# A decoder layer on one core: value products of the self attention in bursts of eight, divisions two runs at a time

## The chip, the cores and the metric

The kernel runs on one NeuronCore of a Trainium2 chip. The metric is the time of one execution on the device in microseconds (us), as the median of several runs; less is better.

The names of the engines in the profile: PE is TensorE (matmuls), PEld its weight loads, DVE is VectorE, ACT is ScalarE, POOL is GpSimd, SP is SyncE, which here issues DMAs.

## The reference

One decoder layer on `x` of shape (4, 1024, 256): a self attention block with residual and layer norm, a cross attention block over 154 context rows with residual and layer norm, and a mixture of 8 experts with a shared expert, residual and layer norm. The change lies in the first attention inside the self attention block:

```python
q = (hidden_states @ Wq + bq).reshape(b, s, NH, HD).transpose(0, 2, 1, 3)
k = (hidden_states @ Wk + bk).reshape(b, s, NH, HD).transpose(0, 2, 1, 3)
v = (hidden_states @ Wv + bv).reshape(b, s, NH, HD).transpose(0, 2, 1, 3)
scores = jnp.einsum('bhqd,bhkd->bhqk', q, k) / jnp.sqrt(jnp.asarray(HD, q.dtype))
mod = jax.nn.sigmoid(hidden_states @ cg_W + cg_b + (cons_vec @ am_W + am_b))
scores = scores * mod.transpose(0, 2, 1)[..., None]
probs = jax.nn.softmax(scores, axis=-1)
ctx = jnp.einsum('bhqk,bhkd->bhqd', probs, v).transpose(0, 2, 1, 3).reshape(b, s, h)
causal_ctx = _mha(hidden_states, hidden_states, ca_Win, ca_bin, ca_Wout, ca_bout, CAUSAL_HEADS)
ctx = ctx * (1.0 - CAUSAL_W) + causal_ctx * CAUSAL_W
meta_ctx = _mha(ctx, ctx, mc_Win, mc_bin, mc_Wout, mc_bout, META_HEADS)
ctx = ctx * (1.0 - META_W) + meta_ctx * META_W
return ctx @ Wo + bo
```

There are 16 heads of 16 features, 1024 queries and 1024 keys per batch, and 4 batches. All is in float32.

## The kernel before, in words

The four batches go through the attention blocks one after the other; the experts follow for all tokens at the end. For each batch the first attention (class `Self`, lines 435 to 559) runs through the loop of lines 932 to 960.

Work is cut by heads and queries. Four heads make a group `g`, 256 queries a part, so a batch has 4 x 4 = 16 units `u` of one group and one part. A unit has 8 steps `s`, so the loop has 128 steps, numbered `n`. The four heads of a group lie 32 partitions apart, so that matmuls with 32 rows each can stand on separate row groups of the array.

In each step the loop does, in this order:

- `maxima(n + 12)`: two matmuls of queries against keys for two heads (L483) into a tile `big` of two PSUM banks (the pool has two such tiles), and a maximum over the keys on DVE (L490). After a unit's eighth step the two halves are joined by DVE into column 31 of each head in `mxcol` (L495); two transposes on TensorE (L397, in `maxima_rows`) turn these columns into rows, and DVE adds them to the query tile (L400), where row 31 of each head is kept for the negative maximum. The lead of 12 steps is done ahead, in `begin`, for the first steps of a batch.
- `exponentials(n)`: four matmuls of keys against queries (L521) for two heads and 256 keys. In even steps they go into two tiles of the pool `one` (three banks), in odd steps into one of these and the single bank `acc`. ACT takes the exponential of each bank (L532) into a tile `ex`. In the last 12 steps of a batch, where there are no maxima left to make, the scores use a `big` tile instead and ACT takes both banks at once (L529).
- in some steps a piece of other work (projections of the next attention, or the end of the previous batch), and then `clock.step()`.

`Clock` keeps a list of pieces that are due: `later(2, f)` runs `f` at the end of the next step, `later(1, f)` at the end of the present one. Three kinds of pieces go through it: the transposed maxima (`rows`), the value products (`product`) and the divisions (`divide`).

The value product (L541) has the weights `v`, 128 keys by 32 columns for a head, 16 features and a column of ones that gives the sum of the exponentials. The four heads write to four column groups of one `one` bank. Before the change a burst covers the exponentials of four steps: 4 chunks of 128 keys by 4 heads, 16 matmuls, behind the steps 3 and 7 of a unit. ACT copies the bank (L549), and for the second half POOL adds the first half to it (L554). Two steps later `divide` transposes the sum (L405, two transposes for 256 queries), and DVE takes the reciprocal of the sums and multiplies (L408, L409).

The tile framework sets semaphores between the engines and places the instructions of each engine in an order of its own, which can differ a little from the order of the program's lines. For example, in the built order one of the two L483 matmuls of a step stands in front of a burst of L541, and the other behind it, once in nearly every unit.

Each matmul in float32 shows as two records in the profile, so `x32` at L541 is a burst of 16.

Of the kernel before, what the change touches and what calls it, by code (L numbers as in the profile page):

```python
# [8 lines left out]
F32 = mybir.dt.float32  # L9
# [3 lines left out]
ALU = mybir.AluOpType  # L13
# [3 lines left out]
P = 128  # L17
# [7 lines left out]
QW = 256  # L25
NG = NH // 4
MH, MD = 4, 64
MR = 31
# [18 lines left out]
def decoder_layer(ctx: ExitStack, tc: tile.TileContext, a, out):  # L47
    nc = tc.nc
# [10 lines left out]
    def big():  # L59
        return pbig.tile([P, 2, 512], F32, tag="big", name="big")  # L60

    def small():
        return pone.tile([P, 512], F32, tag="one", name="one")

    def acc():
        return pacc.tile([P, 512], F32, tag="acc", name="acc")
# [139 lines left out]
    with tc.tile_pool(name="wA", bufs=1) as wA, tc.tile_pool(name="work", bufs=2) as work:  # L206
# [111 lines left out]
        def ex_tile(shape, name):  # L318
            return work.tile(shape, F32, tag="ex", name=name, bufs=EXB)
# [72 lines left out]
        def maxima_rows(mx, q):  # L392

            n = mx.shape[1]
            ps = small()
            for t in range(n):
                nc.tensor.transpose(  # L397
                    ps[:, t * P : (t + 1) * P], mx[:, t].rearrange("p j w -> p (j w)"), ident
                )
            nc.vector.tensor_tensor(q, ps[:, 0 : n * P], q, ALU.add)  # L400

        def divide(avs, g, t0, n, ctok):
            ps = small()
            for t in range(n):
                nc.tensor.transpose(ps[:, t * P : (t + 1) * P], avs[:, t * P : (t + 1) * P], ident)  # L405
            pv = ps[:, 0 : n * P].rearrange("p (t j w) -> p t j w", t=n, w=32)
            rs = work.tile([P, 4, 4], F32, tag="rs", name="rs")
            nc.vector.reciprocal(rs[:, 0:n], pv[:, :, :, HD])  # L408
            nc.vector.tensor_tensor(  # L409
                ctok[:, t0 : t0 + n, g * 64 : (g + 1) * 64].rearrange(  # L410
                    "p t (j d) -> p t j d", d=HD
                ),
                pv[:, :, :, 0:HD],
                rs[:, 0:n].unsqueeze(3).to_broadcast([P, n, 4, HD]),
                ALU.mult,
            )
# [18 lines left out]
        class Self:  # L435
# [35 lines left out]
            def maxima(self, n):  # L471
                u, s = divmod(n, 8)
                g, part = divmod(u, 4)
                st = self.st[g]
                t, kb, pair = s // 4, (s // 2) % 2, s % 2
                if s == 0:
                    st["mxp", part] = work.tile([P, 2, 2, 4], F32, tag="mxp", name="mxp")
                mxp = st["mxp", part]
                ps = big()
                for jj in range(2):  # L480
                    r = 32 * (2 * pair + jj)
                    tok = part * QW + t * P
                    nc.tensor.matmul(  # L483
                        ps[:, jj, :],
                        st["q"][r : r + MR, tok : tok + P],
                        st["k"][r : r + MR, kb * 512 : (kb + 1) * 512],
                        start=True,
                        stop=True,
                    )
                nc.vector.reduce_max(mxp[:, t, kb, 2 * pair : 2 * pair + 2], ps, axis=AX.X)  # L490
                if s == 7:
                    mx = mxcol[u % 2]

                    def rows():
                        nc.vector.tensor_tensor(  # L495
                            mx[:, :, :, MR], mxp[:, :, 0, :], mxp[:, :, 1, :], ALU.max
                        )
                        maxima_rows(mx, st["q"][:, part * QW : (part + 1) * QW])

                    self.clock.later(2, rows)  # L500

            def exponentials(self, n, alone):
                u, s = divmod(n, 8)
                g, part = divmod(u, 4)
                st = self.st[g]
                kcp, pair = s // 2, 1 - s % 2
                if s == 0:
                    st["ex"] = {}
                exs = st["ex"]
                ex = exs[kcp, pair] = ex_tile([P, 2, 512], "ex")  # L510

                if alone:
                    both = big()
                    scs = [both[:, 0, :], both[:, 1, :]]
                else:
                    scs = [small(), small() if s % 2 == 0 else acc()]
                for i in range(2):
                    for jj in range(2):
                        r = 32 * (2 * pair + jj)
                        kc = 2 * kcp + i  # L520
                        nc.tensor.matmul(  # L521
                            scs[jj][:, i * QW : (i + 1) * QW],
                            st["k"][r : r + MR + 1, kc * P : (kc + 1) * P],
                            st["q"][r : r + MR + 1, part * QW : (part + 1) * QW],
                            start=True,
                            stop=True,
                        )
                if alone:
                    nc.scalar.activation(ex, both, AF.Exp, scale=1.0 / HD**0.5)  # L529
                else:  # L530
                    for jj in range(2):
                        nc.scalar.activation(ex[:, jj, :], scs[jj], AF.Exp, scale=1.0 / HD**0.5)  # L532
                if s in (3, 7):

                    def product():
                        av = small()
                        for kc in range(s - 3, s + 1):
                            i = kc % 2 * QW
                            for j in range(4):
                                h = 4 * g + j  # L540
                                nc.tensor.matmul(  # L541
                                    av[32 * j : 32 * j + 32, 0:QW],
                                    self.v[:, kc, h * VW : h * VW + 32],
                                    exs[kc // 2, j // 2][:, j % 2, i : i + QW],
                                    start=(kc == s - 3),
                                    stop=(kc == s),
                                )
                        avs = work.tile([P, QW], F32, tag="avq", name="avq", bufs=3)
                        nc.scalar.copy(avs, av[:, 0:QW])  # L549
                        if s == 3:  # L550
                            st["av"] = avs
                        else:

                            nc.gpsimd.tensor_tensor(avs, avs, st["av"], ALU.add)  # L554
                            self.clock.later(
                                2, lambda: divide(avs, g, 2 * part, 2, self.ctok)
                            )

                    self.clock.later(2, product)
# [19 lines left out]
        def mha_units(qk, v, weight, cx):  # L579
# [93 lines left out]
            for u in range(n + 2):  # L673
                pss = scores(u) if u < n else None
                if 1 <= u <= n:
                    flip(u - 1, 0)
                if u < n:
                    exponentials(u, pss)
                if 1 <= u <= n:
                    flip(u - 1, 1)  # L680
                    del probs[u - 1]
                if u >= 2:
                    product(u - 2)
                yield
# [16 lines left out]
        class Cross:  # L701
# [67 lines left out]
            def product(self, n):  # L769

                g, tp = n // 8, n % 8 // 2
                av = acc()
                pts = [self.pt.pop(n - 1), self.pt.pop(n)]
                for c in range(2):
                    for j in range(4):
                        h = 4 * g + j
                        nc.tensor.matmul(  # L777
                            av[32 * j : 32 * j + 32, 0:QW],
                            self.vx[:, c, h * VW : h * VW + 32],
                            pts[j // 2][0:HK, c, j % 2 * QW : (j % 2 + 1) * QW],  # L780
                            start=(c == 0),
                            stop=(c == 1),
                        )
                avs = work.tile([P, QW], F32, tag="avq", name="avx", bufs=3)
                nc.scalar.copy(avs, av[:, 0:QW])
                self.clock.later(2, lambda: divide(avs, g, 2 * tp, 2, self.ctok))

# [130 lines left out]
        for b in range(B):  # L918
# [13 lines left out]
            for n in range(total):  # L932
                g, s = divmod(n, 32)
# [87 lines left out]
            for g in range(NG):  # L1021
                for c in range(NC2):
# [4 lines left out]
                        start=(c == 0),  # L1027
                        stop=(c == NC2 - 1),
# [10 lines left out]
            for k in range(2):  # L1039
                ps = small()  # L1040
                for c in range(NC2):
# [4 lines left out]
                        start=(c == 0),  # L1046
                        stop=(c == NC2 - 1),
# [76 lines left out]
    def k1(name, shape=(P, NTT, NE)):  # L1124
        return fw.tile(list(shape), F32, tag="k1", name=name, bufs=8)
# [84 lines left out]
    for k in range(2):  # L1210
        mine = k1("mine")
# [257 lines left out]
```

## Time and profile before

| | before |
|---|---|
| time, median of 3 runs | 3394.84 us (3393.89 to 3398.46) |
| the profiled execution's own time | 3315.92 us |
| its span | 3314.1 us |
| granted TensorE clock in it, mean | 0.985 |
| DVE busy | 1668.9 us (50%) |
| ACT busy | 1619.0 us (49%) |
| L490 DVE, maxima over keys | 512 instructions, 611.2 us, mean 1219 ns |
| L541 PE, value products | 4096 records, mean 384 ns each |
| L549 ACT, copies of products | 128 instructions, 47.6 us, mean 372 ns |
| L554 POOL, additions of halves | 64 instructions, 46.4 us, mean 725 ns |

Matmul records overlap in time: the four row groups or column groups work at once. Their durations are modelled and include the way through the array, so that the distance from one start to the next says more than a duration. A window of the profile gives the busy time of each engine in a stretch, and the granted clock, 1.00 for full speed. The self attention loop of the first batch takes from about 80 to 342 us of the span, that of the others some 260 us each from about 740, 1410 and 2080 us.

### The profile page before, as it was taken

The numbers are of one execution on the slowest core, as the hardware profiler recorded it, in microseconds if no ns is written. First come the engines' busy times: TensorE is split into PE (matmuls) and PEld (weight loads), VectorE is DVE, ScalarE is ACT, GpSimd is POOL, SyncE is SP. The second block draws the span as 40 slices with busy tenths as digits, with TensorE's granted clock in tenths as the row PEclk, the third lists the DMA queues.
The fourth block names the chain that finished last, engine by engine and source line by source line (L and its number), as shares of the span: only waits on it lengthen the run. The fifth ranks groups of instructions, "written<-read, shape, count | busy, mean of one in ns | idle before, by whom it ended". The sixth has DMA issues, their size and how long they took to land.

```text
span 3314.1 us, 60483 instructions
## 1 busy us (share of the span) xinstructions
PE 3202.8 (97%) x25064; PEld 2042.6 (62%) x25064; DVE 1668.9 (50%) x3513; ACT 1619.0 (49%) x3179; POOL 352.2 (11%) x565
## 2 busy tenths in 40 slices
PE   8999999999999999999999999999999999999997
PEld 3665667566556675665566756655667575666664
DVE  3665555556655555566545556666456553111113
ACT  1565645465655453756554537555545452233334
POOL 1000000100000001000000010000000004433331
PEclk7999999999999999999999999999999999999998
DMA  7300000101000001010000010000000016322224
GB/s 227 87 1 1 1 1 2 47 28 40 2 1 1 1 2 47 28 39 2 1 1 1 2 47 28 14 2 3 9 10 2 1 42 232 86 48 45 45 46 122
DMA packets 83768, 111.36 MB, mean 34 GB/s; under 512 B 8896, under 2 KB 69672, under 8 KB 83496
## 3 DMA queue, kind: packets, MB, share of 16 engines
q1 hardware_dynamic: 70056, 89.60, 8.6%
q0 software_dynamic: 13440, 17.90, 3.3%
q8 instruction: 200, 3.28, 0.4%
q14 instruction: 72, 0.59, 0.1%
HBM read 59.10 MB, written 48.37 MB: 32 GB/s over the span
## 4 chain that ended last, share of the span: by engine, by line
PE 84%; DVE 10%; issue 3%; ACT 2%; DMA 1%; POOL 0%; SPq 0%; ACTq 0%; DVEq 0%; POOLq 0%
PE big L483 8%; PE big L591 8%; PE big L1293 7%; PE one L627 7%; PE acc L645 7%; DVE mxp L490 7%; PE big L342 7%; PE one L541 7%; PE acc L1319 4%; PE one L521 4%; PE one L758 3%; PE one L356 3%; PE big L191 3%; PE big L723 3%; PE acc L777 2%
## 5 line engine op out<-in xcount | busy, mean ns | idle before, releaser
L490 DVE TENSOR_REDUCE mxp<-big 128x2 f32<-128x1024 f32 x512 | 611.2, 1219 | 344.4 <-PE acc L521 261.4
L483 PE MATMUL big<-k,q 31*128 31x512 f32 x2048 | 615.9, 639 | 34.2 <-DVE mxp L490 23.9
L521 PE MATMUL one<-q,k 32*128 32x256 f32 x2784 | 501.8, 398 | 0.0
L532 ACT ACTIVATE ex<-one 128x512 f32<-128x512 f32 x696 | 390.8, 600 | 218.3 <-PE acc L521 178.0
L323 DVE CUSTOM_DVE_ANT_0 prob<-big,zero_t 128x1024 f32<-128x1024 f32 x256 | 303.6, 1222 | 266.5 <-PE big L591 266.4
L521 PEld LDWEIGHTS one<-q,k 32*128 32x128 f32 x2784 | 331.3, 185 | 33.1 <-ACT ex L532 2.0
L610 ACT ACTIVATE prob<-prob,nmx 128x1024 f32<-128x1024 f32 x256 | 293.0, 1152 | 20.6 <-DVE nmx L323 20.0
L483 PEld LDWEIGHTS big<-k,q 31*128 31x128 f32 x2048 | 186.1, 188 | 175.6 <-DVE mxp L490 88.8
L632 ACT COPY pt<-one 128x512 f32<-128x512 f32 x256 | 137.8, 590 | 305.1 <-PE one L627 305.0
L591 PE MATMUL big<-mk,mq 64*128 64x512 f32 x1024 | 279.3, 623 | 2.6 <-ACT ex L529 2.6
L627 PEld LDWEIGHTS one<-ident,prob 128*128 128x128 f32 x2048 | 219.7, 141 | 96.6 <-issue 90.8
L1293 PE MATMUL big<-wall,xt 128*128 x576 | 270.5, 593 | 0.5 <-ACT xt L1272 0.5
L521 PE MATMUL acc<-q,k 32*128 32x256 f32 x928 | 263.9, 403 | 0.0
L627 PE MATMUL one<-ident,prob 128*128 128x128 f32 x2048 | 255.6, 278 | 0.0
L541 PE MATMUL one<-ex,v 128*32 128x256 f32 x4096 | 250.0, 384 | 5.0 <-DVE q L400 5.0
L1303 DVE TENSOR_TENSOR hidr<-big,slr 128x512 f32<-128x512 f32 x72 | 49.8, 692 | 364.5 <-ACT slr L1301 364.5
L743 ACT ACTIVATE xs<-xs,xmx 128x154 f32<-128x154 f32 x512 | 175.0, 413 | 105.5 <-DVE xmx L323 105.5
L541 PEld LDWEIGHTS one<-ex,v 128*32 128x32 f32 x4096 | 119.9, 110 | 138.6 <-ACT ex L532 54.0
L634 DVE COPY pt<-one 128x512 f32<-128x512 f32 x256 | 164.4, 684 | 9.1 <-PE one L627 9.1
L591 PEld LDWEIGHTS big<-mk,mq 64*128 64x128 f32 x1024 | 98.0, 188 | 100.2 <-issue 78.7
L323 DVE CUSTOM_DVE_ANT_0 xs<-big,bias 128x154 f32<-128x154 f32 x512 | 132.6, 314 | 52.8 <-PE big L723 26.7
L554 POOL TENSOR_TENSOR avq<-avq 128x256 f32<-128x256 f32 x64 | 46.4, 725 | 1050.8 <-ACT avq L549 1050.8
(261 smaller groups left out, 4695.4 us busy)
## 6 DMA issues: line engine op xcount, KB each, us to landing
scratch<-empty SPq DMA_DIRECT2D x1, 9288.0 KB
xg<-scratch SPq DMA_DIRECT2D x72, 129.0 KB
q<-q_rows SPq DMA_DIRECT2D x16, 512.0 KB
k<-k_rows SPq DMA_DIRECT2D x16, 512.0 KB
y<-in_x_dram SPq DMA_DIRECT2D x4, 1024.0 KB
q_rows<-qh SPq DMA_DIRECT2D x8, 512.0 KB
k_rows<-kh SPq DMA_DIRECT2D x8, 512.0 KB
wall<-in_L_ffn_w_gate_dram SPq DMA_DIRECT2D x8, 512.0 KB
```

The costliest lines, as they stand in the source:

```text
L323: nc.vector.tensor_tensor_reduce(out=out, in0=ps, in1=bias, scale=-1.0, scalar=3.0e38, op0=ALU.add, op1=ALU.min, accum_out=low,)
L342: nc.tensor.matmul(ps[:, tb, :], w[:, c, lo : lo + P], xT[:, c, tb * 512 : (tb + 1) * 512], start=(c == 0), stop=(c == NC2 - 1),)
L483: nc.tensor.matmul(ps[:, jj, :], st["q"][r : r + MR, tok : tok + P], st["k"][r : r + MR, kb * 512 : (kb + 1) * 512], start=True, stop=True,)
L490: nc.vector.reduce_max(mxp[:, t, kb, 2 * pair : 2 * pair + 2], ps, axis=AX.X)
L521: nc.tensor.matmul(scs[jj][:, i * QW : (i + 1) * QW], st["k"][r : r + MR + 1, kc * P : (kc + 1) * P], st["q"][r : r + MR + 1, part * QW : ...
L532: nc.scalar.activation(ex[:, jj, :], scs[jj], AF.Exp, scale=1.0 / HD**0.5)
L541: nc.tensor.matmul(av[32 * j : 32 * j + 32, 0:QW], self.v[:, kc, h * VW : h * VW + 32], exs[kc // 2, j // 2][:, j % 2, i : i + QW], start= ...
L591: nc.tensor.matmul(pss[i][:, kb, :], q[r : r + MD, t * P : (t + 1) * P], k[r : r + MD, kb * 512 : (kb + 1) * 512], start=True, stop=True,)
L610: nc.scalar.activation(p, p, AF.Exp, bias=nmx[:, i : i + 1], scale=-1.0, accum_out=sm[:, t % 4, i : i + 1],)
L627: nc.tensor.transpose(ps[:, kc * P : (kc + 1) * P], probs[u][i][:, at : at + P], ident)
L645: nc.tensor.matmul(av[64 * i : 64 * i + 64, (t % 4) * P : (t % 4 + 1) * P], v[:, kc, h * MD : (h + 1) * MD], flipped[u][i][:, kc, :], star ...
L1293: nc.tensor.matmul(ps[:, g, :], xt[:, c * P : (c + 1) * P], wall[:, bass.ds(off + (g * NC2 + c) * D, D)], start=(c == 0), stop=(c == NC2 - 1),
```

## The change

Value products now follow every odd step: `product` takes the two chunks of keys of two steps, 8 matmuls, into a bank of its own, four times in a unit. ACT copies the first of the four into its half of a tile `avq` for two parts (512 columns), the other three into tiles `avp`, which POOL adds on. `divide` runs once for two parts, with four transposes. The transposed maxima are put in the list with `later(1)` in place of `later(2)`, and the joining maximum on DVE follows its reduction at once. The copy of the cross attention (L785) changes its tag, with the same size and number of buffers.

```diff
                 if s == 7:
                     mx = mxcol[u % 2]
-
-                    def rows():
-                        nc.vector.tensor_tensor(
-                            mx[:, :, :, MR], mxp[:, :, 0, :], mxp[:, :, 1, :], ALU.max
-                        )
-                        maxima_rows(mx, st["q"][:, part * QW : (part + 1) * QW])
-
-                    self.clock.later(2, rows)
+                    nc.vector.tensor_tensor(mx[:, :, :, MR], mxp[:, :, 0, :], mxp[:, :, 1, :], ALU.max)
+                    q = st["q"][:, part * QW : (part + 1) * QW]
+                    self.clock.later(1, lambda: maxima_rows(mx, q))
...
-                if s in (3, 7):
+                if s % 2 == 1:
 
                     def product():
+
                         av = small()
-                        for kc in range(s - 3, s + 1):
-                            i = kc % 2 * QW
+                        for i in range(2):
+                            kc = 2 * kcp + i
                             for j in range(4):
                                 h = 4 * g + j
                                 nc.tensor.matmul(
                                     av[32 * j : 32 * j + 32, 0:QW],
                                     self.v[:, kc, h * VW : h * VW + 32],
-                                    exs[kc // 2, j // 2][:, j % 2, i : i + QW],
-                                    start=(kc == s - 3),
-                                    stop=(kc == s),
+                                    exs[kcp, j // 2][:, j % 2, i * QW : (i + 1) * QW],
+                                    start=(i == 0),
+                                    stop=(i == 1),
                                 )
-                        avs = work.tile([P, QW], F32, tag="avq", name="avq", bufs=3)
-                        nc.scalar.copy(avs, av[:, 0:QW])
-                        if s == 3:
-                            st["av"] = avs
-                        else:
-
-                            nc.gpsimd.tensor_tensor(avs, avs, st["av"], ALU.add)
+                        if kcp == 0 and part % 2 == 0:
+                            st["av"] = work.tile([P, 2 * QW], F32, tag="avq", name="avq", bufs=2)
+                        avs = st["av"]
+                        mine = avs[:, part % 2 * QW : (part % 2 + 1) * QW]
+                        if kcp == 0:
+                            nc.scalar.copy(mine, av[:, 0:QW])
+                            return
+                        more = work.tile([P, QW], F32, tag="avp", name="avp", bufs=3)
+                        nc.scalar.copy(more, av[:, 0:QW])
+                        nc.gpsimd.tensor_tensor(mine, mine, more, ALU.add)
+                        if kcp == 3 and part % 2 == 1:
                             self.clock.later(
-                                2, lambda: divide(avs, g, 2 * part, 2, self.ctok)
+                                2, lambda: divide(avs, g, 2 * part - 2, 4, self.ctok)
                             )
...
-                avs = work.tile([P, QW], F32, tag="avq", name="avx", bufs=3)
+                avs = work.tile([P, QW], F32, tag="avp", name="avx", bufs=3)
```

Line numbers in the text are those of the kernel before.

## The prediction

> **What bounds the kernel now.** I read the page first, then the stages in windows, then TensorE, DVE and ACT in order of time over one unit of the self attention (eight steps of the loop at lines 932 to 960).
>
> The page, on the engines' busy time:
>
> ```profile
> PE 3202.8 (97%) x25064; PEld 2042.6 (62%) x25064; DVE 1668.9 (50%) x3513; ACT 1619.0 (49%) x3179; POOL 352.2 (11%) x565
> ```
>
> The window of one unit (us, then busy PE, PEld, DVE, ACT and POOL, then the granted clock):
>
> ```profile
> 200.46:215.68 15.22, 14.48 (x170) 9.07 (x166) 10.24 (x13) 9.15 (x18) 0.73 (x1) 1.00 0.01 2
> ```
>
> The timeline (start, us, engine, line; in brackets the idle time before and what ended it):
>
> ```profile
> 208.16 0.70 PE L483 MATMUL big<-k,q 31*128 31x512 f32 x2 [0.44 <-DVE mxp L490]
> ...
> 210.37 1.93 PE L541 MATMUL one<-ex,v 128*32 128x256 f32 x32
> ...
> 212.23 0.70 PE L483 MATMUL big<-k,q 31*128 31x512 f32 x2
> ...
> 213.41 2.36 DVE L490 TENSOR_REDUCE mxp<-big 128x2 f32<-128x1024 f32 x2 [1.71 <-PE acc L521]
> 213.48 0.60 ACT L532 ACTIVATE ex<-one 128x512 f32<-128x512 f32 x1 [0.69 <-PE acc L521]
> ...
> 213.98 0.59 ACT L532 ACTIVATE ex<-acc 128x512 f32<-128x512 f32 x1
> ...
> 216.12 1.22 DVE L490 TENSOR_REDUCE mxp<-big 128x2 f32<-128x1024 f32 x1
> ...
> 217.37 0.17 DVE L495 TENSOR_TENSOR mxcol<-mxp 128x8 f32<-128x8 f32 x1
> ...
> 217.69 0.41 PE L397 MATMUL one<-ident,mxcol 128*128 128x128 f32 x2 [0.24 <-DVE mxcol L495]
> 218.03 1.12 PE L483 MATMUL big<-k,q 31*128 31x512 f32 x2
> ```
>
> The page says TensorE, and so does the unit, but its 14.48 of 15.22 us are modelled ends. The rows show the pace. A step is the maxima pair (L483) and four score matmuls (L521) on the other two row groups. Where nothing stops them, the first step behind a burst takes 0.98 us (212.23 to 213.21) and the next one 0.87. After each burst of sixteen products (L541, 210.37 to 212.23, 1.86 us) DVE has run dry (idle 1.71 us), and then TensorE waits for DVE, since the maxima have two banks (208.16). From start to start one unit is 1.08 + 1.86 + 0.98 + 1.01 + 0.47 + 1.39 + 1.61 + 0.34 + 1.05 + 1.86 + 0.98 + 1.46 + 1.13 = 15.22 us. The term 1.05 is one maxima matmul that stands alone in front of a burst (218.03 to 219.08), its partner behind it. The interval 15.22 repeats 11 to 12 times in each of four batches.
>
> **The change part by part.** In order, per unit:
>
> Products. The same 4096 records of L541, in four bursts of eight for two of sixteen. A round (a pass of 256 columns; L521's follow each other at 212.57, 212.78, 213.00) takes 0.216 us. A burst of sixteen is eight rounds plus 0.13, so one of eight is 1.00 us and two cost 0.14 more than one. Each new burst also has an entry of 0.11 (the second maxima pass at 209.83 plus 0.43 is 210.26; L541 starts at 210.37).
>
> Wait for exponentials. A burst now needs the exponentials of the step just before, which only one step of work covers. From an odd step's start (212.23) ACT's second exponential (213.98 + 0.59) ends after 2.34 us. TensorE goes on 0.06 us after such an end (an exponential that ended at 326.31, a matmul at 326.37 in the last steps of the batch). So product to product takes 1.00 (burst) + 2.40 = 3.40 us for two steps. Behind the waiting product stand the next maxima and scores, so DVE and ACT wait too. DVE needs 2 x 1.22 us and ACT 4 x 0.5 + 0.37 us in those 3.40: neither is late next. TensorE is, through this latency.
>
> Transposed maxima (L397). The words of the change don't name this: they move one step earlier, behind the very step whose maximum they need. From a step's start DVE begins after 1.18 us (212.23 to 213.41), reduces for 1.22, starts L495 0.03 later, takes 0.17, and TensorE starts 0.15 after that: 2.75 us after the step's start, where it is free after 0.98. Maxima, scores, products, and through them ACT and DVE, queue behind this wait of some 1.6 us. It hides the exponential wait of that pair. The pair takes 2.75 + 0.34 (transposes) + 0.98 + 0.11 + 1.00 = 5.18 us. In return the lone maxima matmul is gone: the built order after the change has 49 such splits fewer, none with a product inside. L400 now stands before the next reduction on DVE; DVE has nothing else there.
>
> Divisions. Per two units one of four transposes for two of two. Two cost 0.34 us (217.69 to 218.03), eight of L135 take 1.09, so 0.14 each; four cost 0.34 + 2 x 0.14 = 0.62 us. They fill the exponential wait, so their pair is 0.98 + 0.87 + 0.14 + 0.62 + 1.00 = 3.61. DVE's reciprocal (0.20) and product (0.29) halve in number; DVE idles there anyway: zero.
>
> Sum of a unit: 2 x 3.40 + 5.18 + (3.40 + 3.61) / 2 = 15.49 against 15.22: 0.27 us more. Times 12 units x 4 batches: +12.7 us.
>
> Costed at nothing, with their cover: 128 more copies on ACT, 128 x 0.372 = 48 us (ACT has over 6 us free per unit; uncovered, 48 us); 128 more additions on POOL, 128 x 0.725 = 93 us (POOL works 0.73 us of 15.22, and the division comes two steps later; uncovered, 0.73 us once per division). The other tag of the cross attention's copy keeps three buffers. SP issues the same 151 instructions in the same order, no DMA is moved past another, and on POOL the memset of the next batch's values still stands before the last addition. Of the four sets of maxima made ahead for the next batch (L397 at 75 and 647 us), the built order shows the first unmoved and the others behind a wait that is over by then: zero.
>
> The last twelve steps of a batch (scores in the wide banks): today they hold waits of 1.10 us for the exponential and 0.99 us for a division; the second goes, the first is partly filled by a product, and three bursts more cost 3 x 0.25. Between -2 and +2 us a batch; I take -0.5, nearest to the rows: -2 us. Together +10.7, say +10 us.
>
> The clock, by two windows that differ after the same idle time, and the row between:
>
> ```profile
> 749.87:753.28 3.41, 1.85 (x12) 0.53 (x8) 3.34 (x11) 2.19 (x4) 0.00 (x0) 1.00 0.01 2
> 753.30:756.69 3.39, 3.29 (x32) 1.38 (x32) 3.12 (x8) 0.46 (x1) 0.00 (x0) 0.50 0.00 0
> 2084.47:2087.88 3.41, 1.73 (x30) 0.94 (x32) 3.38 (x9) 2.30 (x3) 0.00 (x0) 1.00 0.00 0
> ...
> 753.40 3.54 PE L541 MATMUL one<-ex,v 128*32 128x256 f32 x32 [1.68 <-DVE q L400]
> ```
>
> TensorE idled 1.68 us, and the granted clock was 0.50 for the next 3.4 us: the burst took 3.54 us for 1.93. At 2084 us the same idle left the clock at 1.00; there the rest of the stretch was a product on all rows, here half-filled maxima and transposes. The Trainium skill (TensorE: Matmul & The Clock Gate, Why this matters for your kernels) advises against idle gaps above about 3 us only. By the rule the new gap of 1.6 us per unit costs nothing: +10. By the row it may: the gap and its transposes leave about 1.4 us of full matmuls in 3.4 us, between the two cases above. If every fully caught gap, about 0.4 of 48, dropped the clock at 1.6 us each, +31 more. I take the rule's side for the value, since the neighbours are full matmuls as at 2084, and keep +41 as the upper end.
>
> **The rivals.** Faster: the latency is shorter than I read it. If TensorE's first products start on the first exponential and the rest slip in sooner, the pair shrinks; at 3.32 us the unit equals 15.22 (0.27 / 3.5 pairs less), at 3.25 it is 0.25 us shorter, with the last steps gaining 2 us a batch: about -20 us. For it: small bursts keep DVE from running dry for 1.71 and 3.10 us. Against: after the change DVE isn't what TensorE waits for. Slower through the clock: half clock after the new gaps, +25 to +41 us, decided by whether 1.6 us idle with full neighbours suffices; one drop in three speaks for it, 2084 against. Slower through a longer chain: if DVE starts the reduction late, or the product's bank comes free later (it is released by DVE once per unit), each 0.5 us a unit adds 24 us: +35. That the change does nothing is excluded by the built order (four bursts a unit).
>
> **How the numbers follow.** The sum is made against the profiled execution: 3314.1 us span, 3315.92 us time, which becomes 3326. The runs shown have a median of 3394.84, 79 us more, which no row of the profile explains; I carry the difference over unscaled: 3405. Forecast (+10, from -4 to +24): 0.50. Faster chain (-8 to -25): 0.22. Clock: 0.15. Longer chain: 0.13. The range leaves out the ends of both sides: 3376 to 3442. About 0.2%, 7 us, is what a measurement here can tell from no change: faster 0.24, within 0.16, slower 0.60.
>
> **What would show it.** Right: the L400 rows 15.5 us apart in the mean; "L397 waits for DVE" near 1.5 us, 50 times; products waiting about 0.4 us for ACT, three per unit; no lone L483; DVE busy about 10.1 us per unit; granted clock 1.00 in the loop. Wrong: units under 15.2 us (the exponential wait is not there), or a clock under 1.00 within the loop, or waits of L490's banks still ahead of the maxima.

## The result

| | before | after |
|---|---|---|
| time, median of 4 runs | 3396.65 us (3393.89 to 3404.48) | 3431.57 us (3426.87 to 3434.65) |
| the profiled execution's own time | 3315.92 us | 3434.65 us |
| its span, mean granted clock | 3314.1 us, 0.985 | 3432.8 us, 0.970 |

The changed kernel takes 1.0098 of the time of before (95% interval 1.0077 to 1.0119), 35 us more. The forecast was 10 us more, with 3376 to 3442 us as its range: the direction was right and the size about a third of what came. The measured time lies in the range because that was drawn up to the clock rival (+41 us); the forecast's own band ended at +24.

The two profiles on record can't be subtracted as a whole. The one of before lacks a stall of some 70 us in the expert part that all other profiles have (the first experiment), so the comparison goes by stage. From here on, line numbers are those of the kernel that is shown: in the changed kernel the joining maximum is L493, the scores L516, the exponential L527 (L524 for two banks at once), the product L537, the copies L549 and L552, the addition L553.

The page of the changed kernel, engines and one group of instructions (columns: line, engine, operation, shapes, count, then busy us and mean ns, then idle time before and what ended it):

```profile
PE 3200.0 (93%) x25064; PEld 2007.9 (58%) x25064; DVE 1676.5 (49%) x3449; ACT 1659.8 (48%) x3307; POOL 445.0 (13%) x693
...
L553 POOL TENSOR_TENSOR avq<-avq,avp 128x256 f32<-128x256 f32 x192 | 139.2, 725 | 1049.5 <-ACT avp L552 1049.5
```

The counts are those forecast: 128 copies more on ACT and 128 additions more on POOL (192 for 64, 93 us of its time). Neither shows on TensorE's path: POOL waits for copies, nobody for POOL.

Where the time went is seen in the steady part of the loop, ten units of each batch between two L400 rows. First before, then after (columns: the stretch, its length, busy PE, PEld, DVE, ACT and POOL with their counts, granted clock, DMA share, GB/s):

```profile
112.10:264.20 152.10, 144.77 (x1641) 90.81 (x1640) 102.30 (x121) 91.45 (x180) 7.25 (x10) 1.00 0.03 8
```

```profile
115.30:275.90 160.60, 143.22 (x1645) 84.80 (x1648) 104.09 (x111) 97.79 (x200) 21.73 (x30) 0.97 0.03 8
791.30:950.20 158.90, 141.53 (x1644) 84.14 (x1644) 104.07 (x110) 97.69 (x200) 21.73 (x30) 0.98 0.02 8
1466.30:1629.30 163.00, 145.62 (x1644) 85.86 (x1648) 104.11 (x111) 97.91 (x200) 21.72 (x30) 0.95 0.02 8
2145.30:2306.80 161.50, 144.13 (x1644) 85.23 (x1644) 104.07 (x110) 97.79 (x200) 21.72 (x30) 0.96 0.02 8
```

Before, ten units take 152.1 us in every batch at full clock. After, they take 158.9 to 163.0, and never the same: the granted clock is below 1.00. A mean clock of 0.97 over 160.6 us means about 2 x 0.03 x 160.6 = 10 us at half clock. Read from the clock record, the four stretches hold 10.2, 6.8, 15.5 and 12.3 us, 44.8 us in all, as much as 13 pieces of 3.41 us. They lie in 12 of the 40 units; in two of these it is the end of a longer piece (10.24 us) that began in the units before. A unit in which the clock stays up takes 15.32 us, or 15.82 with a division, so 15.57 in the mean. One with a piece of half clock takes 1.6 us more as a rule.

Parts of two units, by the timeline of the changed kernel (start, us, engine, line; in brackets the idle time before):

```profile
203.95 1.51 PE L537 MATMUL one<-ex,v 128*32 128x256 f32 x16
...
207.33 1.52 PE L537 MATMUL one<-ex,v 128*32 128x256 f32 x16
...
211.53 0.41 PE L397 MATMUL one<-ident,mxcol 128*128 128x128 f32 x2 [1.61 <-DVE mxcol L493]
211.87 1.13 PE L483 MATMUL big<-k,q 31*128 31x512 f32 x2
...
213.81 1.83 PE L537 MATMUL one<-ex,v 128*32 128x256 f32 x16
...
224.33 0.63 PE L405 MATMUL one<-ident,avq 128*128 128x128 f32 x4
225.22 1.07 PE L537 MATMUL one<-ex,v 128*32 128x256 f32 x16 [0.26 <-ACT ex L527]
...
228.97 0.41 PE L397 MATMUL one<-ident,mxcol 128*128 128x128 f32 x2 [1.61 <-DVE mxcol L493]
229.31 0.70 PE L483 MATMUL big<-k,q 31*128 31x512 f32 x2
...
230.39 1.07 PE L537 MATMUL one<-ex,v 128*32 128x256 f32 x16
```

The plain pair is there (203.95 to 207.33: 3.38 us), and so is the wait of the transposed maxima, 1.61 us in every unit. After the first of the two waits the maxima take 1.13 us and the burst 1.83; after the second 0.70 and 1.07. The clock, by five windows of that kernel:

```profile
177.86:181.27 3.41, 1.80 (x20) 1.19 (x20) 1.82 (x3) 1.37 (x3) 0.00 (x0) 1.00 0.00 0
181.28:184.69 3.41, 3.41 (x50) 2.11 (x42) 1.92 (x2) 1.97 (x5) 0.73 (x1) 1.00 0.02 5
208.59:212.00 3.41, 1.80 (x24) 1.03 (x22) 1.76 (x4) 1.58 (x4) 0.00 (x0) 1.00 0.00 0
212.00:215.42 3.42, 3.42 (x28) 1.59 (x28) 1.62 (x2) 1.08 (x2) 0.00 (x0) 0.50 0.00 0
225.65:229.06 3.41, 1.80 (x25) 0.94 (x18) 2.21 (x5) 1.47 (x4) 0.00 (x0) 1.00 0.00 0
```

In the window from 208.59 TensorE idles 1.61 us, and the next one is at half clock. Those from 177.86 and 225.65 hold the same idle time and the same 1.80 us of busy time, and the clock stays at 1.00 behind them. By the groups of these windows, 6 product records lie in the one with the drop, none in the first and 12 in the last, so the number of products doesn't decide it.

The drops of this stretch begin at 116.43, 164.22 and 212.00, whole multiples of 3.41 us apart, and every change of the clock in this profile lies on the same grid, as if fixed windows were judged. Of the 40 gaps ahead of the transposes, 23 lie whole inside one window of the grid, and 9 of these were followed by half clock; 17 lie across a border, and none of these was. So in this kernel only gaps that lay whole in a window dropped the clock, and not all of them. What has to be added stays open.

The sum over the four loops, the profile of before against that of after:

| part, four batches | before | after | difference | forecast |
|---|---|---|---|---|
| 40 steady units, clean | 608.3 | 622.7 | +14 | 40 x 0.27 = +11 |
| half clock in them | 0 | 21.3 | +21 | 0 |
| the units behind them, to the last reduction | 216.4 | 227.6 | +11 | +2 |
| last steps behind the last reduction | 122.1 | 125.2 | +3 | -2 |
| first units of a batch | 140.9 | 139.7 | -1 | 0 |
| loops | 1087.8 | 1136.4 | +49 | +11 |

(Clean: the sum of the four windows, 644.0, less 13 x 1.64 for the 44.8 us at half clock.) The stages between the loops take 389 us each in both kernels. The loops show 49 us, the medians 35: the one execution of before that has the stall in its profile took 3385.18 us, 11 less than the median of before, and the profile of after was 3 us over its median. The difference of the medians is the one to trust; the table says how it is divided.

### The profile page after: what moved, and what is told of

It is laid out like the page before. It is cut to its first block, busy times and chain, and to the rows that moved or that the text cites. A ratio compares the mean times of both kernels' runs of the same rounds, so it can differ in the third digit from the quotient of the medians.

```text
span 3432.8 us, 60858 instructions
## 1 busy us (share of the span) xinstructions
PE 3200.0 (93%) x25064; PEld 2007.9 (58%) x25064; DVE 1676.5 (49%) x3449; ACT 1659.8 (48%) x3307; POOL 445.0 (13%) x693
## 4 chain that ended last, share of the span: by engine, by line
PE 88%; DVE 4%; ACT 3%; another core or an unknown queue 2%; issue 1%; DMA 1%; SPq 0%; ACTq 0%; DVEq 0%; POOLq 0%
PE one L537 9%; PE big L483 9%; PE big L591 8%; PE big L1293 7%; PE one L627 7%; PE big L342 7%; PE acc L645 7%; PE one L516 6%; PE acc L1319 4%; PE one L758 3%; PE one L356 3%; PE big L191 3%; DVE mxp L490 3%; PE big L723 2%; PE acc L777 2%
## 5 line engine op out<-in xcount | busy, mean ns | idle before, releaser
L483 PE MATMUL big<-k,q 31*128 31x512 f32 x2048 | 565.8, 650 | 9.7 <-DMA k<-k_rows 4.3
L527 ACT ACTIVATE ex<-one 128x512 f32<-128x512 f32 x696 | 391.7, 603 | 319.3 <-PE acc L516 171.2
L516 PE MATMUL one<-q,k 32*128 32x256 f32 x2784 | 496.9, 397 | 0.8 <-ACT ex L527 0.8
L537 PE MATMUL one<-ex,v 128*32 128x256 f32 x4096 | 343.4, 401 | 22.0 <-ACT ex L524 14.7
L516 PEld LDWEIGHTS one<-q,k 32*128 32x128 f32 x2784 | 313.4, 189 | 29.4 <-ACT ex L527 4.3
L553 POOL TENSOR_TENSOR avq<-avq,avp 128x256 f32<-128x256 f32 x192 | 139.2, 725 | 1049.5 <-ACT avp L552 1049.5
L516 PE MATMUL acc<-q,k 32*128 32x256 f32 x928 | 268.8, 409 | 0.0
L483 PEld LDWEIGHTS big<-k,q 31*128 31x128 f32 x2048 | 173.8, 191 | 146.8 <-issue 118.6
L537 PEld LDWEIGHTS one<-ex,v 128*32 128x32 f32 x4096 | 125.1, 111 | 203.1 <-ACT ex L527 97.8
```

What stands on the lines that cost most here:

```text
L483: nc.tensor.matmul(ps[:, jj, :], st["q"][r : r + MR, tok : tok + P], st["k"][r : r + MR, kb * 512 : (kb + 1) * 512], start=True, stop=True,)
L516: nc.tensor.matmul(scs[jj][:, i * QW : (i + 1) * QW], st["k"][r : r + MR + 1, kc * P : (kc + 1) * P], st["q"][r : r + MR + 1, part * QW : ...
L537: nc.tensor.matmul(av[32 * j : 32 * j + 32, 0:QW], self.v[:, kc, h * VW : h * VW + 32], exs[kcp, j // 2][:, j % 2, i * QW : (i + 1) * QW], ...
```

## The experiments

Line numbers shift with the edits, so the rows shown name the operation too. "Steady units" means the same ten units per batch as above.

### 1. Before once more

No edit. The question was the 79 us between the profile of before and its runs.

> The kernel before, once more, for its profile. Theory: the first profile of before (span 3314.1 us) lacks a stall of some 70 us in the expert part that its timed runs (3394 us) have, and that the profile after shows at 2836 to 2905 us. Then this profile has a span of 3380 to 3400 us with the stall in it, and units of the self attention of 15.22 us again. Rival: the timed runs are longer all over (a lower clock): then the units are longer than 15.22 us in this profile.

3385.18 us in one run. The steady units take 15.22 us again, and the loops 1088.0 us against 1087.8. The difference lies in the expert part, which takes 1038.7 us here and 969.2 in the first profile. Two groups of that part, first in the profile on record, then in this one (busy us, mean ns, then idle before):

```profile
L191 PE MATMUL big<-x2T,shwca 128*128 128x512 f32 x144 | 67.5, 601 | 0.9 <-ACT x2T L138 0.9
...
L135 PE MATMUL big<-ident,y1again 128*128 128x128 f32 x16 | 1.9, 273 | 0.0
```

```profile
L191 PE MATMUL big<-x2T,shwca 128*128 128x512 f32 x144 | 69.5, 617 | 31.0 <-ACT x2T L138 31.0
...
L135 PE MATMUL big<-ident,y1again 128*128 128x128 f32 x16 | 6.1, 384 | 30.1 <-issue 30.1
```

TensorE issues sixteen transposes with 30 us of idle time that no semaphore explains, and then idles another 31 us. The changed kernel (28.6 and 34.3 us) and all experiments have it as well, with an expert part of 1038 to 1047 us. The two parts shift against each other, 14 to 30 us and 30 to 51 us, 60 to 65 us together. It is no part of this change, and its cause was not tried. So the true base was 3394 us, and carrying the 79 us over unscaled was right.

### 2. The transposed maxima back in their old place

The changed kernel with the old `rows`, bursts of eight and divisions together kept:

```diff
-                    nc.vector.tensor_tensor(mx[:, :, :, MR], mxp[:, :, 0, :], mxp[:, :, 1, :], ALU.max)
-                    q = st["q"][:, part * QW : (part + 1) * QW]
-                    self.clock.later(1, lambda: maxima_rows(mx, q))
+                    def rows():
+                        nc.vector.tensor_tensor(
+                            mx[:, :, :, MR], mxp[:, :, 0, :], mxp[:, :, 1, :], ALU.max
+                        )
+                        maxima_rows(mx, st["q"][:, part * QW : (part + 1) * QW])
+                    self.clock.later(2, rows)
```

> The change with the transposed maxima put back (due two steps later, joined then). Theory (the early transposes leave TensorE idle for 1.6 us a unit, and that lowers the clock): no half clock in the steady units, a unit of about 15.4 us, total 10 us over before (ratio 1.003), some 25 us under the changed kernel. Rival (the bursts of eight, with their waits for exponentials, lower the clock and make the loss): half clock stays at over 30 us in the steady units and the ratio to before stays near 1.010.

3414.51 us, 1.0055 of before (1.0039 to 1.0072). One of its windows, and the rows around the transposes:

```profile
788.80:944.00 155.20, 146.43 (x1642) 86.73 (x1640) 102.19 (x111) 97.52 (x200) 21.76 (x30) 1.00 0.03 8
```

```profile
206.72 0.41 PE L397 MATMUL one<-ident,mxcol 128*128 128x128 f32 x2 [0.75 <-DVE mxcol L495]
207.06 1.12 PE L483 MATMUL big<-k,q 31*128 31x512 f32 x2
208.11 1.07 PE L542 MATMUL one<-ex,v 128*32 128x256 f32 x16
```

The wait is 0.75 us for 1.61 and the clock stays at 1.00, but the lone maxima matmul is back (207.06, with a burst at 208.11). A unit takes 15.52 us, as much as a clean one of the changed kernel, 15.57. A unit was expected at 15.4 us and the total 10 us over before; it came to 20. So moving the transposes earlier trades the lone matmul for a longer wait at no gain, as the forecast had it; what it costs beyond that is the clock. This kernel's drops are gone from the steady units, and it is 17 us faster than the changed one.

### 3. The early transposes alone

The kernel before, with bursts of sixteen, and only the edit of the transposed maxima (`later(1)`, joined at once), the reverse of the diff in experiment 2.

> The kernel before with the transposed maxima early (due one step later, joined at once), bursts of sixteen and divisions as before. Theory (the early transposes are the loss): the lone maxima matmul goes (1.05 us less), the wait of 1.6 us comes, a clean unit is about 15.3 us, and half clock appears in 10 to 15 units of 40; total 20 to 35 us over before (1.006 to 1.010). Rival (the bursts of eight are the loss): clock 1.00 in the units, total within 8 us of before or below it.

3446.48 us, 1.0151 of before (1.0134 to 1.0168). Two of its four windows:

```profile
113.60:274.10 160.50, 141.03 (x1644) 86.54 (x1646) 104.27 (x121) 92.19 (x180) 7.26 (x10) 0.95 0.02 8
790.10:953.80 163.70, 144.22 (x1644) 87.51 (x1646) 104.30 (x121) 92.18 (x180) 7.27 (x10) 0.93 0.02 8
```

One clean unit takes 15.26 us, nearly what it took before (15.22), and yet ten take 160.5 to 163.7: 82.9 us at half clock, as much as 24 pieces of 3.41 us. The total is 52 us over before, where 20 to 35 were expected: this one edit loses more than the whole change. Its gaps ahead of L397 are 1.44 us, shorter than in the changed kernel, so the length of one gap isn't the measure alone. Nor is it only whether the gap lies whole in a window of the grid: of 11 that lie across a border, 4 dropped the clock here. TensorE also waits 0.45 us for DVE elsewhere in the unit, which may add to it; that was not tried apart.

### 4. The gap filled

The changed kernel with two matmuls more ahead of the transposed maxima, 512 and 256 columns, into the bank that the transposes overwrite. They add work and change nothing else:

```diff
-        def maxima_rows(mx, q):
+        def maxima_rows(mx, q, busy):
...
+            nc.tensor.matmul(ps, ident, busy[:, 0:512], start=True, stop=True)
+            nc.tensor.matmul(ps[:, 0:QW], ident, busy[:, 0:QW], start=True, stop=True)
...
-                    self.clock.later(1, lambda: maxima_rows(mx, q))
+                    self.clock.later(1, lambda: maxima_rows(mx, q, st["k"]))
```

> The changed kernel with two matmuls more ahead of the transposed maxima, into the bank that these overwrite (512 and 256 columns, 0.86 + 0.43 us of TensorE), so that TensorE works in its wait of 1.6 us. Theory (half clock follows from the idle gap): no half clock in the steady units, all units at 15.3 and 15.8 us, 15 to 30 us less than the changed kernel, although TensorE does 80 us more. Rival (TensorE's work is what counts, or the clock falls for another reason): units longer by up to 1.3 us, 60 us more, or half clock as before.

3422.67 us, 1.0087 of before (1.0062 to 1.0111). One window, and its timeline at the transposes (L396 and L397 are the two added matmuls; the transposes follow at 222.23):

```profile
788.20:943.20 155.00, 153.40 (x1684) 89.65 (x1685) 104.07 (x111) 97.47 (x200) 21.73 (x30) 1.00 0.02 8
```

```profile
220.65 1.12 PE L396 MATMUL one<-k,ident 128*128 128x512 f32 x2
221.61 0.59 PE L397 MATMUL one<-k,ident 128*128 128x256 f32 x2
```

More work in the gap, and ten units take 155.0 us in every batch, at clock 1.00: 620.1 us for 40 units against 644.0. That is the evidence that the varying part of the change's cost is the clock and that the idle gap sets it off. (The two matmuls end the idle time and put work on all rows in its place; these runs don't part the two.) The total came down by 9 us only; the stages between the loops took 390 to 393 us in its profile instead of 389, which gives some of it back, for a reason that these runs don't show.

### 5. The transposes later

The changed kernel with `later(3)` for the transposes, the maximum still joined at once:

```diff
-                    self.clock.later(1, lambda: maxima_rows(mx, q))
+                    self.clock.later(3, lambda: maxima_rows(mx, q))
```

> The changed kernel with the transposed maxima due three steps later (still joined at once), where DVE has their maximum long ready and no product stands in the same step. Theory (the loss of the change is the place of these transposes, by their wait and by the clock): no idle gap of 1.6 us, clock 1.00 in the units, no lone maxima matmul, a unit of 3 x 3.38 + 3.55 + 0.25 = 13.9 us, some 65 us under before (ratio 0.981). Rival (the bursts of eight lose by themselves, through the waits for exponentials): the units stay at 15.2 us or more.

3363.65 us, 0.9910 of before (0.9893 to 0.9927). Units of 14.10 and 14.60 us, 14.35 in the mean, longer than expected (13.9), and the total is 31 us under before for the 65 expected. Two rows of its waits (engine and line, what it waited for: us in total, times, longest):

```profile
PEld one L537 <- ACT ex L527: 22.2, 64, 0.5
...
PEld one L537 <- DVE q L400: 4.0, 12, 0.3
```

L397 waits no more, and no maxima matmul stands alone. Left is the products' wait for exponentials, 64 times, and a new one: the burst behind the transposes waits 0.3 us for L400, which now stands behind a reduction on DVE.

### 6. The products later as well

```diff
-                    self.clock.later(2, product)
+                    self.clock.later(3, product)
```

> As the run before it, and the products also due three steps later, so that two steps of work lie between a step's scores and the product of their exponentials. Theory (what is left between two products, 3.38 us, is the latency of the exponentials): the wait goes, a pair of steps takes 0.98 + 0.87 + 0.11 + 1.00 = 2.96 us, a unit 12.6 us, about 130 us under before (0.962). Rival (ACT or the banks bound it: ACT works some 10 us a unit, and the product's bank comes later): the unit stays between 13.3 and 13.9 us.

3273.88 us, 0.9647 of before (0.9631 to 0.9663): 121 us under the kernel before, where some 130 were expected. Window and timeline:

```profile
750.10:880.10 130.00, 129.75 (x1644) 82.22 (x1640) 103.15 (x111) 95.66 (x200) 21.80 (x30) 1.00 0.03 10
```

```profile
205.59 1.07 PE L537 MATMUL one<-ex,v 128*32 128x256 f32 x16
...
208.53 1.07 PE L537 MATMUL one<-ex,v 128*32 128x256 f32 x16
```

A plain pair is 2.93 us (expected 2.96) instead of 3.38, and TensorE is busy for 129.75 of 130.00 us. The burst record is 1.07 us long and no longer 1.51, since both exponentials are there when it starts. Units take 12.71 and 13.29 us, 13.00 in the mean (expected 12.6): one pair in each unit still takes 3.38.

### 7. The same two moves with bursts of sixteen

The kernel before with the transposes at `later(3)`, joined at once; then with the products at `later(3)` as well.

> The kernel before, bursts of sixteen and divisions of one run, with the transposed maxima due three steps later and joined at once. Theory (the lone maxima matmul of 1.05 us and the transposes' wait cost before too): a unit of 13.3 to 13.9 us, 65 to 95 us under before (0.972 to 0.981). Rival (DVE running dry behind bursts of sixteen is what bounds it): over 14.5 us a unit.

> The kernel before with transposed maxima and products both due three steps later, in bursts of sixteen. It tells what bursts of eight are worth where neither waits. If the burst's length matters through DVE running dry: a unit of 13.0 to 13.6 us, longer by 0.4 or more than with bursts of eight in the same places. If not: within 0.3 us of it, or under it, since two bursts of eight cost 0.25 more on TensorE than one of sixteen.

3320.93 us, 0.9780 (0.9763 to 0.9796), units of 13.86, within what was expected; and 3340.67 us, 0.9845 (0.9826 to 0.9864), units of 14.14, where 13.0 to 13.6 was expected. With bursts of sixteen the second move loses. A row of the second kernel's waits and two of DVE's timeline say why:

```profile
PEld big L483 <- DVE mxp L490: 17.8, 36, 0.9
```

```profile
200.30 4.81 DVE L490 TENSOR_REDUCE mxp<-big 128x2 f32<-128x1024 f32 x4 [2.02 <-PE one L516]
206.82 2.36 DVE L490 TENSOR_REDUCE mxp<-big 128x2 f32<-128x1024 f32 x2 [1.72 <-PE one L516]
```

Behind each burst of sixteen (1.86 us) DVE has run dry, 2.02 and 1.72 us per unit, and later TensorE waits for DVE to free a bank of maxima. The waits of this row come to 17.8 us between 100 and 270 us of the span, against 8.2 us with the transposes moved alone, and to 0.8 us with bursts of eight in the same places (experiment 6). There a unit takes 13.00 us for 14.14. The divisions are joined there too; with bursts of eight and divisions apart it is 13.12 (experiment 8), so the shorter bursts are worth 1.02 us a unit. Burst length and position have to be taken together:

| transposes, products | bursts of sixteen | bursts of eight, divisions together |
|---|---|---|
| early, 2 steps later | 1.0151 | 1.0098 (the change) |
| as before, 2 | 1 (before) | 1.0055 |
| 3 steps later, 2 | 0.9780 | 0.9910 |
| 3 steps later, 3 | 0.9845 | 0.9647 |

### 8. The divisions apart

The changed kernel with a division for each run of queries; and the same edit on top of experiment 6:

```diff
-                        if kcp == 3 and part % 2 == 1:
+                        if kcp == 3:
                             self.clock.later(
-                                2, lambda: divide(avs, g, 2 * part - 2, 4, self.ctok)
+                                2, lambda: divide(mine, g, 2 * part, 2, self.ctok)
```

> The changed kernel, with the division taken per run of queries again: two transposes of two divisions each instead of one transpose of four and one DVE pass. Bursts of eight and early transposed maxima stay. In the built order a maxima matmul stands alone behind the two transposes of a division again. Theory: the lone maxima matmul costs its 1.05 us (less what the exponential's wait behind it hides, at most 0.9), four transposes against eight per two units are equal in number: a unit of 15.7 to 16.3 us where the change has 15.56 without clock drops, +7 to +35 us on the changed kernel, no drop of the clock more than there. Rival: the divisions together were worth nothing, since DVE and the exponential's wait cover both forms: a unit of 15.5, the total within 7 us of the changed kernel.

> Transposed maxima three steps behind their maxima and products three steps behind their scores, in bursts of eight, and in addition the division taken per run of queries (two transposes each) instead of two runs together. No maxima matmul stands alone in the built order. Theory: with no split pair, two transposes per unit cost what four per two units cost on TensorE: units of 13.0 us within 0.1, alternating no more (13.0 and 13.0 for 12.7 and 13.3), total within 7 us of 3274. Rival: the second division puts a wait of its own into every unit (DVE's reciprocal and product between a transpose and the next reduction): units of 13.3, +14 us.

3512.34 us, 1.0357 (1.0336 to 1.0377), 81 us over the changed kernel: more than either theory gave. Some 40 us of it lie in the steady units. The clean unit is 16.42 us, 0.85 more, and the steady stretches hold 58 us at half clock, 13 more (here all 16 gaps that lie whole in a window dropped it, and none of the 24 others). The rows of the first:

```profile
212.29 0.41 PE L405 MATMUL one<-ident,avq 128*128 128x128 f32 x2
212.75 1.12 PE L483 MATMUL big<-k,q 31*128 31x512 f32 x2
213.80 1.07 PE L537 MATMUL one<-ex,v 128*32 128x256 f32 x16
```

With two transposes instead of four, the framework again sets one maxima matmul alone in front of the burst (212.75 to 213.80, 1.05 us), now behind L405. The pair takes 4.95 us where the changed kernel's takes 3.38 without and 4.33 with a division. In the late version no matmul stands alone: 3283.78 us, 0.9677 (0.9657 to 0.9696), units of 13.12 in every case for 13.00 in the mean, between theory and rival. So the joint divisions as such are worth about 0.1 us a unit, and 0.85 us where they keep a matmul from standing alone.

## Why the prediction was right or wrong

**Products in bursts of eight, and the wait for exponentials.** Right: 3.38 us for a plain pair against 3.40. The latency is the cause, since products one step later take 2.93.

**Transposed maxima.** The wait was right, 1.61 us against "some 1.6", and so was the trade: the lone matmul's 1.05 us for it, no gain (15.57 against 15.52 in experiment 2). That the lone matmul goes because these transposes move holds for bursts of sixteen (experiment 3). For bursts of eight it was half of it: experiment 8 has them moved and one matmul alone again, so there it takes the joint division as well.

**The unit.** Forecast 15.49, measured 15.57, from terms that were off in both directions. A burst behind a plain pair starts on the first exponential and waits inside for the second (1.51 for 1.07 us), which moves 0.45 us into the pair behind it. So the pair with the transposes took 5.62 behind a plain pair and 5.17 behind a division, 5.40 in the mean, for a forecast 5.18, and the next one 2.94 for 3.40. The pair with the division took 4.33 for 3.61: the four transposes are 0.63 us as forecast, and of the 0.72 us more, 0.45 is that shift and 0.26 idle time: the burst starts at 225.22, on the end of the exponential that began at 224.56. That one belongs to the step ahead, which fits a `one` bank that has to come free because the division took one; it was not tried apart.

**The clock: the step that failed.** The prediction showed the row against itself, 1.68 us of idle time and half clock behind it, and then took the side of the Trainium skill's rule (TensorE: Matmul & The Clock Gate, Why this matters for your kernels), which warns of gaps above about 3 us. It put the term at 0. In the runs, gaps of 1.61 us brought 44.8 us at half clock into 12 of 40 units, which cost 21 us, the largest term of all; with the gap filled, the half clock was gone (experiment 4). The measurement decides against the rule here. The rival that carried this term gave +25 to +41 us and had a chance of 0.15, and a clock under 1.00 within the loop was among the prediction's own signs of being wrong.

The rival's price was right (1.6 us a piece). Its rate, 0.4 of the gaps, came near the 12 of 40 by luck: it lets every fully caught gap drop the clock, and of 23 caught whole only 9 did. The argument that the neighbours "are full matmuls as at 2084" was wrong: within 3.41 us around the gap most of the busy time is maxima and scores, of 31 or 32 rows each, and transposes. But the products don't explain the drops either, since windows without any of them kept the clock.

**Last steps and last units.** Forecast -2 us, measured +3 for the last steps; where the clock stays up, a batch's last steps take 30.5 us for 29.5, so even the sign of this small term was wrong. The units just ahead, with other work among them, gave +11 for +2; their parts were not taken to pieces.

**What was costed at nothing** held: POOL's additions and ACT's copies are on nobody's path, the middle stages kept their 389 us. **The faster-chain rival** (0.22) did not come, as the plain pair was 3.38 and the rival needed under 3.32. Half of its mechanism did: the burst starts on the first exponential, but then waits inside for the second.

## What to carry to other kernels

A piece of work that waits for another engine's answer belongs as many steps later as the answer takes; here two steps more for the transposes and one for the products turned a loss of 1% into a gain of 3.5%. With the products in their old place, the shorter bursts lost in two of the three rows of the table. When a change opens an idle gap on TensorE at each pass of a loop, believe a row of the trace that shows the clock falling after such a gap more than a rule about longer ones, and move the waiting work or fill the gap. An order written by a scheduler can split a pair of 31-row matmuls around a burst, at a whole microsecond; look at the built order for it after each edit: here it went with the whole change, and came back with the transposes in their old place and with the divisions apart.

## What was not expected of the hardware

- A TensorE idle time of 1.4 to 1.6 us halved the clock for the next 3.4 us again and again: 44.8 us at half clock, in 12 of 40 units of the changed kernel, and 82.9 us in 40 units with the early transposes alone. Which gap is hit follows a fixed grid of 3.41 us, at least in part. With 0.75 us (experiment 2) it never did in 40 units, nor with the gap filled.
- A wait of the kind that one trace calls "issue" cost TensorE 14 to 30 us over sixteen transposes in the expert part, and a wait behind them another 30 to 51, some 60 to 65 us together, in every profile but the first of before. What brings it about stays open.
